# A shift by whole columns: read from DRAM at a computed place instead of multiplied by a matrix

## The chip, the cores and the metric

The kernel runs on one core of a Trainium2 chip. The metric is the device time of one execution in microseconds (us). The engines are called as in the profile: PE is TensorE, DVE is VectorE, ACT is ScalarE, POOL is GpSimd, SP is SyncE, whose queue issues almost all transfers (DMA) of this kernel. All arithmetic is in f32.

## The reference

Four layers follow each other on x with shape (32, 192, 56, 56). Each adds the result of a convolution-like block to x, and each block reads x through a group norm (32 groups of 6 channels, mean and variance over the 6 channels and all pixels of an image).

```python
x = x + _L0_conv_ref(_gn(x), ...)   # attention over 49 agents per image, 6 heads
x = x + _L1_conv_ref(_gn(x), ...)   # a scan over the 3136 pixels, forwards and backwards
x = x + _L2_conv_ref(_gn(x), L2_conv_offset)
x = x + _L3_conv_ref(_gn(x), ...)   # a 55x55 filter per channel, through a Fourier transform
```

Layer 2 is the one that the change is about. Its 48 positions own four channels each. A position has an offset in x and y; its whole part R shifts the image, with zeros where the source lies outside, and its fraction gives a 3x3 filter, a product of a column part and a row part, that is applied to the shifted image:

```python
R = jnp.round(offset); Ri = R.astype(jnp.int32)
y_src = jnp.arange(Hn)[None, :] - Ri[:, 1:2]
x_src = jnp.arange(Wn)[None, :] - Ri[:, 0:1]
out = where the source exists: inp[:, :, y_src, x_src], else 0
delta = offset - R
sq = (f[None, None, :] + delta[:, 0, None, None]) ** 2 + (f[None, :, None] + delta[:, 1, None, None]) ** 2
kern = jnp.exp(-sq / (2.0 * SIGMA ** 2)); kern = kern / kern.sum(axis=(1, 2), keepdims=True)
out_LO = depthwise convolution of out with kern, padding 1
```

The offsets are an input of the kernel, so the place is known only when it runs.

## The kernel before

The program has three long parts on the same core, one after the other. `attention` does layer 0 image by image, from about 300 to 5200 us of the span (before it, `make_filter` turns the filter of layer 3 into `spectra`). `scan_pairs` does layer 1 in pairs of images, up to about 8300 us, and writes its result to a tensor `x2` in DRAM, laid out by channel. `channel_blocks` does layers 2 and 3 channel by channel in the rest. It is called the channel stage here.

**Layout.** A channel of `x2` is a tile of 114 partitions: for each of two interleaved sets of images, 56 rows and one more row that holds the image's group mean (spread by the scan). Along the free axis lie 16 images of 56 columns each, 896 numbers. `rs2` holds the norm's factor for each channel and image.

**Shift (`shift`).** Two matrices, made on POOL once for each position (`matrices`, every fourth channel), carry shift, filter and zeros: one for rows (`diff_y`, then multiplied on PE by the fixed matrix `lags`, which subtracts the mean row, `L1550`, and copied by DVE, `L1552`), one for columns (`diff_x`). Each matrix takes three taps (`L1542`) and two additions (`L1546`, `L1547`) on POOL. A channel is then taken through PE twice, two interleaved images at a time: eight matmuls (`L1589`) give the rows shifted and the image turned, with columns on the partitions; DVE multiplies this by the norm's factor on its way out of PSUM (`L1596`); eight more (`L1607`) shift the columns and turn it back; DVE adds it to x (`L1615`) and sums x (`L1616`) for the next norm.

**Norm of layer 3 (`centre`).** DVE subtracts the mean into `padded` (`L1633`), ACT squares (`L1635`), DVE sums the squares (`L1636`); PE adds over the six channels of a group (`means`, `L1624`).

**Layer 3.** `analyse` takes `padded` to spectra (PE `L1757`, ACT copies `L1763`, PE `L1655`) and DVE multiplies with the filter's spectrum in six operations for each of three batches (`L1662` to `L1668`). `synthesise` goes back (PE `L1681` with ACT copies `L1688`, PE `L1698`), DVE multiplies by the norm's factor (`L1700`) and adds to x (`L1701`), and SP stores two halves of the channel (`L1704`).

**Order of the work.** The loop runs over 32 groups of six channels, with six steps each. In a step, one channel of the group before is analysed, the one before that is synthesised, and the present group has two shifts (steps 0 to 2) or two centrings (steps 3 to 5). The parts are generators and a written list says how they alternate:

```python
two = [shift(q, 2 * j + i) if j < 3 else centres(q, 2 * j - 6 + i) for i in range(2)]
for step in (taking, two[0], two[0], taking, ending, ending, two[0], taking, ...):
    next(step, None)
```

The framework may then reorder instructions on each engine within what the data and the buffers allow; every engine works through its own list in order. PSUM has eight banks here: four of the tag `ps`, shared by shift, `analyse` and `synthesise`, and two each for `re` and `im`. There are 15 buffers for x.

Of the kernel before, what the change touches and what calls it, by code (L numbers as in the profile page):

```python
# [67 lines left out]

def _resize_matrix():

    at = (np.arange(S) + 0.5) * POOL / S - 0.5
    w = np.maximum(0.0, 1.0 - np.abs(at[:, None] - np.arange(POOL)[None, :]))
    return w / w.sum(1, keepdims=True)
# [5 lines left out]
    (114, (114,)), (112, (112,)), (114, (2,)),  # L79
# [3 lines left out]
def _constants():  # L83
# [16 lines left out]
    for t in range(2):  # L100
# [17 lines left out]
        "chan_k": _filled([f[n] for n in "f1 f2 f3 f4 ones_rows lags diff_y diff_x at_rows".split()]),  # L118
# [3 lines left out]
def _spectral_constants():  # L122
# [21 lines left out]
    for s in range(2):  # L144
# [7 lines left out]
    col = np.arange(2 * S) % S  # L152
    together = np.arange(2 * S)[:, None] // S == np.arange(2 * S)[None, :] // S
    diff_x = np.where(together, col[None, :] - col[:, None], 1e6)
    at_rows = np.stack([np.concatenate([col, [0, 0]]), row], 1)
# [8 lines left out]
        "diff_x": diff_x,  # L164
        "at_rows": at_rows,
# [199 lines left out]
def attention(ctx: ExitStack, tc: tile.TileContext, a, ready, x1, st_a, st_c):  # L365
# [48 lines left out]
    for t in (*agents_b[0], *agents_b[1], v_a, v_c):  # L414
        nc.gpsimd.memset(t, 0.0)

# [342 lines left out]
    for b in range(NB):  # L759
# [28 lines left out]
        for t in range(1, NK + 2):  # L788
# [21 lines left out]
            if more and t == 4:  # L810
                o[0] = convolve(0)
                normed(nxt, rs, nb, 3)
        nc.sync.dma_start(out=st_a[:, b % 2, b // 2], in_=st[:, 0])
# [37 lines left out]
def scan_pairs(ctx: ExitStack, tc: tile.TileContext, a, k, x1, st_a, st_c, x2, rs2, count):  # L851
# [86 lines left out]
    kept_a, kept_c = small("kept_a", [128, 2, NB // 4, 2]), small("kept_c", [128, 2, NB // 4])  # L938
# [261 lines left out]
    def conclude(s):  # L1200
# [3 lines left out]
        nc.vector.tensor_copy(kept_a[:, p % 2, p // 2, :], rs[:, 0:2, 0])  # L1204
        nc.vector.tensor_copy(kept_c[:, p % 2, p // 2 : p // 2 + 1], rs[:, 2])
# [46 lines left out]
    for i, r in enumerate((slice(0, 64), slice(64, 128))):  # L1252
        nc.sync.dma_start(out=rs2[128:C, :, :, i], in_=kept_c[r])
# [17 lines left out]
def scan_guarded(ctx: ExitStack, tc: tile.TileContext, a, k, x1, x2, rs2):  # L1271
# [45 lines left out]
    kept = cp.tile([T, 2, 2, NB // 4, 2], F32, name="kept", tag="kept")  # L1317
# [47 lines left out]
    for b in range(NB):  # L1365
# [84 lines left out]
        g, i = b // 4, b // 2 % 2  # L1450
        nc.vector.tensor_copy(kept[:, :, i, g, b % 2], rs)
# [11 lines left out]
def channel_blocks(ctx: ExitStack, tc: tile.TileContext, a, k, x2, rs2, spectra, out):  # L1463
# [30 lines left out]
    f1, f2, f3, f4, ones, lags, diff_y, diff_x, at = pieces  # L1494
# [3 lines left out]
    for t in padded:  # L1498
        nc.gpsimd.memset(t[:, :, S:64], 0.0)

# [17 lines left out]
    ok = cp.tile([PR, NP, 2], F32, name="ok", tag="ok")  # L1518
    for d in range(2):
        nc.vector.tensor_scalar(ok[:, :, d], rnd[:, :, d], at[:, d : d + 1], None, ALU.add)  # L1520
    low = cp.tile([PR, NP, 2], F32, name="low", tag="low")
# [3 lines left out]
    nc.vector.tensor_tensor(gs, gs, _bc(ok.rearrange("p n d -> p (n d)"), [PR, NP * 2, 3]), ALU.mult)  # L1525
    where = cp.tile([PR, NP * 2, 3], F32, name="where", tag="where")
    for f in range(3):
        nc.vector.tensor_scalar(where[:, :, f], rnd.rearrange("p n d -> p (n d)"), float(1 - f), None, ALU.add)
# [3 lines left out]
    def matrices(n):  # L1532

        if n in made:
            return made[n]
        got = []
        for d, diff in ((1, diff_y), (0, diff_x)):
            r, m = diff.shape
            t = [wp.tile([r, m], F32, name=f"tap{d}{f}", tag=f"tap{d}{f}", bufs=1) for f in range(3)]
            for f in range(3):  # L1540
                i = 2 * n + d
                nc.gpsimd.tensor_scalar(  # L1542
                    t[f], diff, where[:r, i, f : f + 1], gs[:r, i, f : f + 1], ALU.is_equal, ALU.mult
                )
            mat = wp.tile([r, m], F32, name=f"mat{d}", tag=f"mat{d}", bufs=3)
            nc.gpsimd.tensor_tensor(t[0], t[0], t[1], ALU.add)  # L1546
            nc.gpsimd.tensor_tensor(mat, t[0], t[2], ALU.add)  # L1547
            if d == 1:
                ps = pp.tile([128, BANK], F32, name="ps", tag="ps", bufs=4)
                nc.tensor.matmul(ps[:PR, :PR], lags, mat, start=True, stop=True)  # L1550
                mat = wp.tile([r, m], F32, name="mat2", tag="mat2", bufs=3)
                nc.vector.tensor_copy(mat, ps[:PR, :PR])  # L1552
            got.append(mat)
        made.clear()
        made[n] = got
        return got
# [7 lines left out]
    def begin(n):  # L1564
        q = Group()
        q.n, q.x, q.padded = n, [], []
        q.scale = sp.tile([2 * S, GROUP, NG, 2], F32, name="scale", tag="scale")
        for i in range(2):
            nc.sync.dma_start(
                out=q.scale[S * i : S * (i + 1)], in_=rs2[n * GROUP : (n + 1) * GROUP, i].partition_broadcast(S)  # L1570
            )
# [4 lines left out]

    def shift(q, j):

        c = q.n * GROUP + j
        rows, cols = matrices(c // 4)  # L1580
        x = xp.tile([PR, NI, S], F32, name="x", tag="x")
        nc.sync.dma_start(out=x, in_=x2[c].rearrange("s h g w -> (s h) g w"))
        flat = x.rearrange("p g w -> p (g w)")
        turned = wp.tile([2 * S, NG, 2, S + 1], F32, name="turned", tag="turned")
        for g0 in range(0, NG, 4):
            n = min(4, NG - g0)
            ps = psum()
            for g in range(n):
                nc.tensor.matmul(  # L1589
                    ps[: 2 * S, g * PR : (g + 1) * PR],  # L1590
                    flat[:, (g0 + g) * 2 * S : (g0 + g + 1) * 2 * S],
                    rows,
                    start=True,
                    stop=True,
                )
            nc.vector.tensor_tensor(  # L1596
                turned[:, g0 : g0 + n].rearrange("p g s h -> p (g s) h"),
                ps[: 2 * S, : n * PR].rearrange("p (g h) -> p g h", h=S + 1),
                _bc(q.scale[:, j, g0 : g0 + n].rearrange("p g s -> p (g s)"), [2 * S, 2 * n, S + 1]),
                ALU.mult,  # L1600
            )
        yield
        for g0 in range(0, NG, 4):
            n = min(4, NG - g0)
            ps = psum()
            for g in range(n):
                nc.tensor.matmul(  # L1607
                    ps[:PR, g * 2 * S : (g + 1) * 2 * S],
                    turned[:, g0 + g].rearrange("p s h -> p (s h)"),
                    cols,  # L1610
                    start=True,
                    stop=True,
                )
            xc = flat[:, g0 * 2 * S : (g0 + n) * 2 * S]
            nc.vector.tensor_tensor(xc, xc, ps[:PR, : n * 2 * S], ALU.add)  # L1615
# [15 lines left out]
    def centre(q, j):  # L1631
        t = padded[(q.n * GROUP + j) % len(padded)]
        nc.vector.tensor_tensor(t[:, :, 0:S], q.x[j], _bc(q.mean, [PR, NI, S]), ALU.subtract)  # L1633
        sq = wp.tile([PR, NI, S], F32, name="sq", tag="sq")
# [73 lines left out]
    def centres(q, j):  # L1708
# [5 lines left out]
        yield  # L1714
# [3 lines left out]
    before, ending = None, iter(())  # L1718
    for n in range(C // GROUP + 1):
        q = begin(n) if n < C // GROUP else None  # L1720
        for j in range(GROUP):
# [4 lines left out]
            for step in (  # L1726
                taking, two[0], two[0], taking, ending, ending, two[0], taking, ending, ending, two[1], two[1], taking,
                ending, two[1], ending,
            ):
                next(step, None)  # L1730
            for rest in (*two, taking, ending):
# [37 lines left out]
def all_blocks(ctx: ExitStack, tc: tile.TileContext, a, k, out):  # L1769
# [7 lines left out]
    x1, x2 = scratch("x1", [NB, C, N]), scratch("x2", [C, 2, S + 1, NB // 2, S])  # L1777
# [118 lines left out]
```

## Time and profile before

| | us |
|---|---|
| median of 3 runs | 12296.9 |
| lowest and highest | 12290.89, 12297.15 |
| the profiled execution, its own time | 12294.66 |
| its span, from first to last instruction | 12292.8 |
| mean granted clock of TensorE | 0.966 |

| busy share of the span | PE | weight loads | DVE | ACT | POOL |
|---|---|---|---|---|---|
| whole program | 92% | 58% | 88% | 50% | 18% |

The 16 DMA engines moved 719.69 MB in 930055 packets, of which 770325 were under 512 bytes. The page gives each engine's busy time in 40 slices of the span (one slice is 307 us); the channel stage begins in slice 28. In it the granted clock is 1.00 (window 9000 to 11000 us). Lines such as `L1589` are lines of the kernel before. In groups of instructions the last columns are busy us, mean ns of one, idle time of the engine just before them and what ended it; in a timeline the first two columns are start and duration in us. An f32 matmul shows as two records.

### The profile page before, as it was taken

The numbers are of one execution on the slowest core, as the hardware profiler recorded it, in microseconds if no ns is written. First come the engines' busy times: TensorE is split into PE (matmuls) and PEld (weight loads), VectorE is DVE, ScalarE is ACT, GpSimd is POOL, SyncE is SP. The second block draws the span as 40 slices with busy tenths as digits, with TensorE's granted clock in tenths as the row PEclk, the third lists the DMA queues.
The fourth block names the chain that finished last, engine by engine and source line by source line (L and its number), as shares of the span: only waits on it lengthen the run. The fifth ranks groups of instructions, "written<-read, shape, count | busy, mean of one in ns | idle before, by whom it ended". The sixth has DMA issues, their size and how long they took to land. (4 is left out here: it accounts for less than half of the span.)

```text
span 12292.8 us, 164375 instructions
## 1 busy us (share of the span) xinstructions
PE 11329.2 (92%) x62734; PEld 7107.7 (58%) x62734; DVE 10836.4 (88%) x15489; ACT 6205.0 (50%) x11808; POOL 2250.7 (18%) x2228
## 2 busy tenths in 40 slices
PE   7999999999999999788888888888999999999999
PEld 3555555655555555333333333336777777777777
DVE  6888888888888887999999999997888888888888
ACT  3555555555555554566666666663333333333333
POOL 0000000000000000655555555551000000000000
PEclk9999999999999999999999999999999999999999
DMA  2111111111111111244344433442111111111111
GB/s 69 40 42 46 52 41 40 40 40 40 40 40 40 42 50 44 75 103 100 95 97 103 101 94 97 103 101 65 44 41 45 41 44 42 44 42 44 42 43 29
DMA packets 930055, 719.69 MB, mean 59 GB/s; under 512 B 770325, under 2 KB 807236, under 8 KB 920124
## 3 DMA queue, kind: packets, MB, share of 16 engines
q1 hardware_dynamic: 919020, 683.39, 21.7%
q10 hardware_dynamic: 10240, 25.70, 0.8%
q8 instruction: 500, 8.19, 0.3%
q14 instruction: 295, 2.42, 0.1%
HBM read 403.47 MB, written 240.65 MB: 52 GB/s over the span
## 5 line engine op out<-in xcount | busy, mean ns | idle before, releaser
L572 DVE SCALAR_TENSOR_TENSOR o<-v_a,att_w,o 128x896 f32<-128x896 f32 (+1 forms) x1024 | 1053.8, 1029 | 418.6 <-ACT v_a L546 291.5
L1763 ACT COPY y<-ps 64x252 f32<-64x252 f32 (+1 forms) x2376 | 808.2, 340 | 1135.0 <-PE ps L1757 1104.8
L1681 PE MATMUL ps<-fixed,real 84*84 84x112 f32 x6144 | 1090.9, 259 | 0.0
L1681 PE MATMUL ps<-fixed,imag 84*84 84x112 f32 x6144 | 1089.5, 259 | 0.0
L1688 ACT COPY z<-ps 84x448 f32<-84x448 f32 x768 | 405.6, 528 | 1218.5 <-PE ps L1681 1217.0
L1086 POOL MEMSET f<- 128x1 f32 x96 | 8.9, 99 | 4726.3 <-DMA st_c<-st 4721.3
L1681 PEld LDWEIGHTS ps<-fixed,real 84*84 84x84 f32 x6144 | 784.0, 153 | 134.2 <-issue 95.8
L1681 PEld LDWEIGHTS ps<-fixed,imag 84*84 84x84 f32 x6144 | 763.8, 153 | 0.0
L1079 ACT ACTIVATE q<-q 128x784 f32<-128x784 f32 x384 | 328.2, 855 | 802.5 <-DVE q L1074 633.1
L834 PE MATMUL ps<-sq,fixed 128*128 128x392 f32 x512 | 297.3, 743 | 428.6 <-ACT sq L1157 428.6
L572 DVE SCALAR_TENSOR_TENSOR o<-v_c,att_w,o 128x448 f32<-128x448 f32 (+1 forms) x1024 | 635.0, 620 | 5.1
L585 PE MATMUL ps<-xs_a,gk_a 128*98 128x448 f32 (+1 forms) x1536 | 637.1, 495 | 0.0
L589 ACT ACTIVATE pr<-ps,low 98x896 f32<-98x896 f32 (+1 forms) x384 | 352.3, 918 | 559.9 <-DVE low L587 559.9
L586 PE MATMUL ps<-xs_c,gk_c 125*98 125x448 f32 (+1 forms) x1536 | 631.6, 492 | 0.0
L1547 POOL TENSOR_TENSOR mat<-tap,tap 114x114 f32<-114x114 f32 x96 | 40.8, 425 | 3166.1 <-PE ps L1607 2313.2
L677 PE MATMUL ps<-gq_a,xs_a 128*112 128x294 f32 x1792 | 602.8, 417 | 19.2 <-DVE pq L682 19.2
L1698 PE MATMUL ps<-z,fixed 84*114 84x448 f32 x1536 | 608.8, 539 | 0.0
L834 PE MATMUL ps<-x,weights 128*128 128x392 f32 x1536 | 577.4, 519 | 27.5 <-DVE bv L1108 14.2
L678 PE MATMUL ps<-gq_c,xs_c 125*112 125x294 f32 x1792 | 594.5, 412 | 0.0
L1655 PE MATMUL re<-y,fixed 128*84 128x420 f32 (+1 forms) x1152 | 532.3, 543 | 8.7 <-ACT y L1763 7.6
L1655 PE MATMUL im<-y,fixed 128*84 128x420 f32 (+1 forms) x1152 | 526.9, 538 | 0.0
L690 ACT ACTIVATE pq<-pq 112x1176 f32<-112x1176 f32 x224 | 265.3, 1184 | 498.9 <-DVE pq L682 376.0
(367 smaller groups left out, 29245.2 us busy)
## 6 DMA issues: line engine op xcount, KB each, us to landing
x<-x SPq DMA_DIRECT2D x576, 392.0 KB
x<-x SPq DMA_DIRECT2D x512, 196.0 KB
x<-x SPq DMA_DIRECT2D x192, 399.0 KB
out_x<-x SPq DMA_DIRECT2D x384, 196.0 KB
x<-in_x SPq DMA_DIRECT2D x32, 1568.0 KB
x<-x SPq DMA_DIRECT2D x32, 1568.0 KB
x<-in_x SPq DMA_DIRECT2D x64, 392.0 KB
rd<-rd ACTq DMA_DIRECT2D x128, 196.0 KB
```

The source lines that it names most:

```text
L572: nc.vector.scalar_tensor_tensor(dst, tap(i), dww[:, t, i : i + 1], dst, ALU.mult, ALU.add)
L585: mm(ps[P2, h, :n], g[:, cols], xs_a[j][:, px], start=True, stop=False)
L586: mm(ps[P2, h, :n], gk_c[0:KC, 2 * j + h, cols], xs_c[j][0:KC, px], start=False, stop=True)
L589: nc.scalar.activation(pr[:, :, :n], ps[P2, :, :n], AF.Exp, bias=low[:, j, p : p + 1], accum_out=sums[:, j, p : p + 1])
L677: mm(ps[:SUB, i, :HA], xs_a[j][:, px], g, start=True, stop=False)
L678: mm(ps[:SUB, i, :HA], xs_c[j][0:KC, px], gq_c[0:KC, 2 * j + (q + i) // ns], start=False, stop=True)
L834: mm(out, aa, srcs[t][h], start=True, stop=False)
L1655: nc.tensor.matmul(ps[:, : n * 84], f2[:, i, :], y[:, i0 : i0 + n].rearrange("p g s u -> p (g s u)"), start=True, stop=True)
L1681: nc.tensor.matmul(ps[:84, i * 2 * S : (i + 1) * 2 * S], part[:, i0 + i].rearrange("p s u -> p (s u)"), f3[:, m, :], start=(m == 0), stop= ...
L1688: nc.scalar.copy(z[:, i0 : i0 + n].rearrange("p g m w -> p (g m w)"), ps[:84, : n * 2 * S])
L1698: nc.tensor.matmul(got, f4[:, m, :], z[:, i0 : i0 + n, m, :], start=(m == 0), stop=(m == 1))
L1763: nc.scalar.copy(y[64 * m : 64 * m + 64, 2 * g0 + i : 2 * (g0 + n) : 2], got[64 * i : 64 * i + 64, :, :, m, :])
```

## The change

The columns are no longer shifted by a matrix. `x2` is now one flat tensor in DRAM in which each row of 56 numbers is followed by 56 zeros (`PITCH`), with 64 zeros ahead and behind (`LEAD`). A whole channel read from a start moved by R columns is then the channel shifted by R columns, with zeros coming in. The zeros (`gaps`) are written by 192 DMAs in `attention`, six behind each image's code.

For each channel a new function `prepare` runs four channels ahead: SP loads the start from SBUF into a register once for each position, a DMA reads the channel from the computed place into one of three buffers `shifted`; POOL multiplies it by the norm's factor (`scale`, now laid out by images on the free axis); ACT multiplies it by the three column taps, each with its own scale (`y`, then twice `more`, from a shared set of three buffers `spare`, which the squares of `centre` use too); POOL adds the three into `smooth`. In `shift`, PE applies the row matrix with two matmuls of 448 columns, and DVE adds the result to x. x itself is loaded too, as before, but from the layout with gaps. The row matrix (`matrix`) is made as before, the column matrix falls away, and with it the multiplication on DVE (`L1596`). The list of steps loses one turn for each shift. `kept_a`, `kept_c`, `kept` and `rs2` follow the new order of images.

```diff
+PITCH = 2 * S
+LEAD = 64
...
+    for at in (0, x2.shape[0] - LEAD):
+        nc.sync.dma_start(out=x2[at : at + LEAD].unsqueeze(0), in_=zeros[0:1])
...
+        for c in range(C * b // NB, C * (b + 1) // NB):
+            nc.sync.dma_start(
+                out=gaps[c].rearrange("s h g w -> (s h) g w"),
+                in_=zeros[:, 0:S].unsqueeze(1).to_broadcast([2 * (S + 1), NB // 2, S]),
+            )
...
+    shifted = [cp.tile([PR, NI, S + 2], F32, name=f"shifted{i}", tag=f"shifted{i}") for i in range(3)]
+    for t in shifted:
+        nc.gpsimd.memset(t, 0.0)
...
+    begins = cp.tile([1, NP], I32, name="begins", tag="begins")
+    nc.vector.tensor_scalar(begins, rnd[0:1, :, 0], -1.0, float(LEAD), ALU.mult, ALU.add)
...
+    def prepare(c):
...
+        n, j = divmod(c, GROUP)
+        if j == 0:
+            scales[n] = sp.tile([PR, GROUP, NI], F32, name="scale", tag="scale", bufs=3)
...
+        i = c // 4
+        if c % 4 == 0:
+            begin_at[i] = nc.values_load(
+                begins[0:1, i : i + 1], engines=(mybir.EngineType.SP,), min_val=LEAD - S, max_val=LEAD + S
+            )
+        t = shifted[c % len(shifted)]
+        there = flat_x2[bass.ds(begin_at[i] + c * SPAN, SPAN)].rearrange("(p g w) -> p g w", p=PR, w=PITCH)
+        nc.sync.dma_start(out=t[:, :, 1 : S + 1], in_=there[:, :, 0:S])
+        nc.gpsimd.tensor_tensor(t, t, _bc(scales[n][:, j], [PR, NI, S + 2]), ALU.mult)
+        y = wp.tile([PR, NI, S], F32, name="smooth", tag="smooth", bufs=5)
+        taps = [gs[:, 2 * i, f : f + 1] for f in range(3)]
+        nc.scalar.activation(y, t[:, :, 0:S], AF.Copy, scale=taps[0])
+        for f in (1, 2):
+            more = wp.tile([PR, NI, S], F32, name="more", tag="spare", bufs=3)
+            nc.scalar.activation(more, t[:, :, f : f + S], AF.Copy, scale=taps[f])
+            nc.gpsimd.tensor_tensor(y, y, more, ALU.add)
+        smooth[c] = y
+
     def shift(q, j):
...
-        for g0 in range(0, NG, 4):
...
-                nc.tensor.matmul(
-                    ps[: 2 * S, g * PR : (g + 1) * PR],
-                    flat[:, (g0 + g) * 2 * S : (g0 + g + 1) * 2 * S],
-                    rows,
...
-            nc.vector.tensor_tensor(
-                turned[:, g0 : g0 + n].rearrange("p g s h -> p (g s) h"),
...
-                nc.tensor.matmul(
-                    ps[:PR, g * 2 * S : (g + 1) * 2 * S],
-                    turned[:, g0 + g].rearrange("p s h -> p (s h)"),
-                    cols,
...
+        for g0 in range(0, NI, 8):
+            n = min(8, NI - g0)
+            px = slice(g0 * S, (g0 + n) * S)
             ps = psum()
+            nc.tensor.matmul(ps[:PR, : n * S], rows, y[:, px], start=True, stop=True)
+            nc.vector.tensor_tensor(flat[:, px], flat[:, px], ps[:PR, : n * S], ALU.add)
         nc.vector.tensor_reduce(q.sums[:, 0, j, :], x, AX.X, ALU.add)
...
+    for c in range(4):
+        prepare(c)
...
+            prepare(n * GROUP + j + 4)
...
+    n = C * 2 * (S + 1) * (NB // 2) * PITCH
+    x1, flat = scratch("x1", [NB, C, N]), scratch("x2", [n + 2 * LEAD])
+    wide = flat[LEAD : LEAD + n].rearrange("(c s h g w) -> c s h g w", c=C, s=2, h=S + 1, w=PITCH)
+    x2, gaps = wide[..., 0:S], wide[..., S:PITCH]
```

## The prediction

> **What bounds the kernel now.** I read the 40 slices of the page first: PE reads 9 over the last third, which is the channel stage. Then the busy times of an undisturbed stretch of that stage, the groups in the same stretch by shape, and PE's timeline.
>
> ```profile
> PE   7999999999999999788888888888999999999999
> DVE  6888888888888887999999999997888888888888
> POOL 0000000000000000655555555551000000000000
> ```
>
> The next line holds a window, its length, then the busy us of PE, weight loads, DVE, ACT and POOL, the granted clock, the DMA share and GB/s.
>
> ```profile
> 9000.00:11000.00 2000.00, 1975.96 (x13516) 1525.41 (x13515) 1737.21 (x2917) 714.49 (x1718) 164.00 (x245) 1.00 0.17 43
> ```
>
> One reduction `L1616` belongs to one channel and it counts 99, so a channel takes 2000/99 = 20.2 us: PE works 99% of it, DVE 17.55 us, ACT 7.2, POOL 1.7. PE sets the pace. The starts of `L1757` in PE's timeline, one per step of the loop, stand 23.2, 23.2, 23.2, 17.6, 16.4 and 17.7 us apart: three steps with two shifts each, three with two centrings each, 121.3 us for a group of six channels, 32 groups.
>
> ```profile
> 10012.46 1.74 PE L1589 MATMUL ps<-mat,x 114*112 114x114 f32 x16
> 10014.22 1.02 PE L1607 MATMUL ps<-mat,turned 112*114 112x112 f32 x8
> 10015.08 1.01 PE L1655 MATMUL re<-y,fixed 128*84 128x504 f32 x2
> 10015.93 0.96 PE L1607 MATMUL ps<-mat,turned 112*114 112x112 f32 x8
> 10016.73 1.01 PE L1655 MATMUL im<-y,fixed 128*84 128x504 f32 x2
> 10017.58 3.17 PE L1698 MATMUL ps<-z,fixed 84*114 84x448 f32 x8
> 10020.58 2.44 PE L1757 MATMUL ps<-fixed,padded 114*128 114x168 f32 x16
> ```
>
> From start to start: `L1589` holds PE 1.76 us, `L1607` 0.86 + 0.80 = 1.66 us. Eight records with 448 columns (`L1698`) hold it 3.00 us, so 0.375 each; an f32 matmul is two records.
>
> **PE's part of the change.** Per channel 16 small matmuls (3.42 us) go and two with 448 columns come (4 x 0.375 = 1.50 us): 1.92 us less, 3.84 in a step with two shifts. The lags matmul stays. PE's floor for a group is 3 x (23.2 - 3.84) + 51.7 = 109.8 us against 121.3; if all of it arrived, 32 x 11.5 = 368 us.
>
> **DVE, ACT, POOL, DMA.** These rows are the groups of the same 2000 us by shape (last numbers: busy us, mean ns).
>
> ```profile
> L1596 DVE TENSOR_TENSOR turned<-ps,scale 112x456 f32<-112x456 f32 x198 | 124.2, 630 | 107.8 <-PE ps L1589 107.8
> L1701 DVE TENSOR_TENSOR x<-x,o 114x448 f32<-114x448 f32 x198 | 123.6, 624 | 1.9
> L1664 DVE TENSOR_TENSOR real<-a,a 84x420 f32<-84x420 f32 x199 | 117.7, 591 | 0.0
> L1633 DVE TENSOR_TENSOR padded<-x,mean 114x896 f32<-114x896 f32 x99 | 106.9, 1080 | 0.6
> L1635 ACT ACTIVATE sq<-padded 114x896 f32<-114x896 f32 x99 | 94.1, 951 | 37.3 <-DVE padded L1633 35.7
> L1542 POOL TENSOR_SCALAR tap<-fixed,where,gs 112x112 f32<-112x112 f32 x72 | 65.3, 912 | 5.0
> L1546 POOL TENSOR_TENSOR tap<-tap,tap 114x114 f32<-114x114 f32 x25 | 10.7, 428 | 0.0
> ```
>
> DVE loses `L1596`: 124.2/99 = 1.25 us per channel, leaving 16.3, or 97.8 per group: about 16.4 us in a step with shifts, 16.2 in one with centrings (two shifts keep 4.6 us in `L1615` and `L1616`, two centrings 4.3 in `L1633` and `L1636`). ACT gains three passes over 114x896 at 0.95 (`L1635`), 2.9 us: 10.1 of 18 us, room enough in sum. POOL loses the three taps and two adds of the column matrix every fourth channel, and gains per channel one multiplication over 928 and two additions over 896 elements. The trace has no such long POOL operation. A one-element copy of the scan takes 0.18 us where nothing stands beside it, the addition over 114 takes 0.428; that makes 2.2 ns an element, so 2.13 us for 896 and 2.2 for 928. Bounds: 0.83 us from the memset `L302` (952 ns for 1024, no reads) and 3.4 us with 428 ns in full proportion. I take 2.13, since it separates the fixed part. POOL then works 6.5 us plus 0.8 for the row matrix, 7.3 of some 18 per channel: no bound as a sum.
>
> Each channel gets a second load of x2, now in runs of 224 bytes like the output stores. DMA is busy 17% in this stage; with the x load in runs of 224 bytes too, a channel then has three transfers of the stores' kind instead of one, and the stores are now some 10 of the 17%: about 35%, hidden. In the order of SP they stand behind output stores that wait for `L1701`'s addition; they run at least two steps ahead of their use. The 192 zero fills of the attention stage (399 KB each) run while DMA is at 16%, but some 36 to 42 of them stand in one row on SP ahead of `gk_c`, needed once per image (146 us): I price that, with the longer first chain load, POOL, ACT, POOL, PE, at 25 us; 0 and 60 are the ends.
>
> **The shared wait.** What decides is where POOL and DVE touch. The scan shows it: line, count, then ns least/median/most.
>
> ```profile
> L1073 POOL COPY b<-p x157: 185/1662/2577, 5599.5 to 8298.0; 128x1 f32<-128x1 f32 x157
> L1664 DVE TENSOR_TENSOR real<-a,a x298: 579/582/702, 9001.9 to 10999.4; 84x420 f32<-84x420 f32 x99, 84x504 f32<-84x504 f32 x50
> ```
>
> One element is copied in 0.185 us or, typically, in 1.66, ending as a DVE operation with two inputs in SBUF ends. The other way round, `L1664` (two SBUF inputs) rises from 0.582 to 0.70 only when it begins 0.2 us after a tap of POOL. [...]
>
> In numbers of this trace: DVE has nine operations with two SBUF inputs per channel (`L1664` and `L1668` three each, `L1701` two, `L1633`), 597/99 = 6.0 us, so between two of them lie (16.3 - 6.0)/9 = 1.14 us of other work. If a POOL operation of 2.13 us holds off the next one to its end, as DVE's hold off the copies, that one loses 2.13 - 1.14 = 1.0 us. Ends: 0.12 (`L1664`) and 2.13 (all of it). I take 1.0, because the 0.12 was lost beside an operation over 112 elements, not 896.
>
> Where they fall matters. In the order of the changed kernel POOL's 18 long operations of a group are not spread: ten fall into the first step with shifts, two into the other two, six into the steps with centrings. DVE in the first step: 16.4 + 10 = 26.4 us, above PE's 19.4. ACT agrees: five passes named `more` stand ahead of that step's twelve copies of `y`, held by their three buffers until POOL's additions free them (the fifth may write only after two additions, 5.2 us), and a later one stands ahead of a copy of `z`; walking that chain with 2.3 us per POOL operation gives a first step of some 24 us, so the two explanations overlap and I count the larger. The next two steps: PE's 19.4 each. Centring steps: 16.2 + 2 = 18.2 against PE's 17.2. Sum 26.4 + 38.8 + 54.6 = 119.8. Two engines so close lose to each other: the stage loses 0.24 us per channel now with PE well ahead, I add 0.3, 1.8 per group. 121.6 against 121.3: 32 x 0.3 = 10 us more, and 25 from above. The profiled execution took 12294.66 us (span 12292.8), 2.2 under the median of 12296.9. Forecast 12294.7 + 35 = 12330 us. With 0.7 to 1.3 us per operation (first step not under 24.2) its own range is 12200 to 12480.
>
> **Rivals.** *PE stays the bound* (faster). POOL delays DVE by 0.12 us as at `L1664`, and the ACT chain costs the first step 3.6 us: 23 + 38.8 + 51.7 = 113.5, minus 7.8 x 32 = 250, plus 25: about 12070; all of PE's saving gives 11950. For it: the only row in which DVE waits for POOL is small, and DVE has 2 us to spare per channel. Against it: the copies. It decides once the delay is below 0.5 us per operation (DVE then 21.4 us in the first step, 17.2 in the centring ones).
>
> [...] POOL's next operation is issued before the waiting DVE operation gets its turn, as `L1073` shows copies of 2577 ns that wait out more than one DVE operation. At 1.6 us per operation: 32.4 + 38.8 + 58.2 + 1.8 = 131.2, plus 317 + 25: 12640; at 2.13, 12890. It decides from 1.3 us on.
>
> *The shifted copy comes late*: SP's in-order queue puts its load behind a store, and PE waits for it. One lost step per group would be 18 x 32 = 580 us; the two steps of lead speak against it.
>
> **Chances.** Forecast 0.45, PE bound 0.27, POOL again 0.25, late copy 0.03. The measurement tells about 0.2% (25 us) from no change. Faster: 0.27 and 0.10 of the forecast's low part, 0.37; same 0.08; slower 0.55. Range 12000 to 12680: about 0.07 of the PE case lies below, 0.12 of the slow ones above.
>
> **What would show it.** Right: `L1664`, `L1668` and the addition into x with means well above 0.59 and 0.62; a POOL addition near 2.1 us; first step of a group near 26 us, centring steps near 18; PE under 95% busy. PE at 98% with steps of 19.4 and 17 would refute the shared wait; DVE's means doubled would make the second rival. Wrong altogether: waits of the `smooth` matmul for DMA, or an attention stage longer by over 60 us.

## The result, and the profile after

The changed kernel takes 12731.8 us (median, 12730.91 to 12735.85) against 12296.72 us beside it: a ratio of 1.0356, interval 1.0338 to 1.0374. That is 435 us slower. The forecast was 12330 us, with a range of 12000 to 12680. Each kernel's runs lie within 7 us of each other.

The 40 slices of the page after, to be held against those of before: PE reads 5, 4, 4 in the second to fourth slice, where it read 9. That is the attention stage, which the change touches only with the zero fills. In the last third PE reads 8 and 9, DVE has risen to 9, and POOL reads mostly 3 and 4, where it read 0.

```profile
PE   7544999999999999978888888887899999999999
DVE  6444888888888888799999999997899999999998
POOL 0000000000000000055555555554533433433330
```

The profiled execution (span 12729.3 us, before 12292.8) splits by the starts of four instructions: the first scan operation (`L1072` before, `L1080` after), the first matmul with the row matrix and `lags` (`L1550`, `L1556`), and the first and the last of the 192 steps. A step begins with the forward DFT's matmul (`L1757`, `L1767`).

| stretch | before, us | after, us | difference |
|---|---|---|---|
| start to the first scan operation (attention) | 4919.3 | 5429.4 | +510 |
| from there to the first matmul with `lags` | 3466.7 | 3460.2 | -7 |
| from there to the first step | 35.0 | 70.8 | +36 |
| first step to last step | 3839.7 | 3736.5 | -103 |
| rest | 32.1 | 32.4 | 0 |

**The attention stage.** The first line below is a group of the page: its last part is PE's idle time in front of `L589`, 451 us (0.0 in front of the same matmul before), and what ended it. The second view is the DMA queue of SP: start, us, instruction, how many. The third is the same queue before.

```profile
L589 PE MATMUL ps<-xs_c,gk_c 125*98 125x448 f32 (+1 forms) x1536 | 637.9, 496 | 451.0 <-DMA gk_c<-once 451.0
```

```profile
515.42 0.94 SPq L522 DMA_DIRECT2D gq_c<-once  x1
516.42 217.83 SPq L817 DMA_DIRECT2D x<-zeros  x37
734.35 5.79 SPq L522 DMA_DIRECT2D gk_c<-once  x1
```

```profile
647.38 0.92 SPq L519 DMA_DIRECT2D gq_c<-once  x1
766.54 0.89 SPq L519 DMA_DIRECT2D gk_c<-once  x1
```

37 zero fills stand between the load of `gq_c` and that of `gk_c`, and SP is 218 us in getting rid of them, 5.8 us each. In the queue of before 119 us lie between these two loads, so there was cover for some 119 us. PE waits for `gk_c` in four of the first images, for 128, 108, 105 and 105 us, 446 in all: the loads of `gk_c` stand 280, 268, 268, 263 and 154 us apart, then mostly 146.7 us as before. What the other 64 of the 510 us are is not split further; the granted clock from 480 to 760 us is 0.77, where it was 0.97.

**The channel stage.** An undisturbed stretch, with the columns of the line that the prediction shows: PE has fallen from 1976 to 1889 us, DVE has risen from 1737 to 1868, POOL from 164 to 749, the DMA share from 0.17 to 0.31. PE sets the pace no longer.

```profile
9000.00:11000.00 2000.00, 1889.25 (x11001) 1315.35 (x11000) 1868.34 (x2786) 1028.85 (x2070) 749.29 (x436) 0.98 0.31 66
```

One group, step by step, in the same columns:

```profile
10147.70:10171.70 24.00, 21.40 (x110) 13.65 (x110) 23.86 (x29) 13.42 (x25) 21.32 (x11) 0.93 0.48 103
10171.70:10193.10 21.40, 19.65 (x111) 13.25 (x110) 19.25 (x31) 8.26 (x18) 6.57 (x7) 1.00 0.23 50
10193.10:10212.50 19.40, 19.15 (x109) 13.09 (x108) 16.60 (x29) 7.23 (x17) 0.00 (x0) 1.00 0.21 43
10246.40:10264.90 18.50, 17.43 (x114) 12.89 (x112) 18.46 (x28) 10.93 (x22) 7.55 (x4) 1.00 0.32 65
```

These are the three steps with shifts and the last one with centrings. In the first POOL works 21.3 us and DVE is full (23.86 of 24.00). In the third POOL does nothing, and PE's matmuls take nearly the whole step: 19.4 us, the floor of the prediction. The groups by shape of another 2000 us show who pays; the last two lines are the 84x504 forms before:

```profile
L1608 POOL TENSOR_TENSOR smooth<-smooth,more 114x896 f32<-114x896 f32 x204 | 461.0, 2263 | 948.7 <-ACT more L1607 933.8 <-ACT smooth L1604 6.5
L1709 DVE TENSOR_TENSOR x<-x,o 114x448 f32<-114x448 f32 x204 | 190.2, 932 | 2.3
L1672 DVE TENSOR_TENSOR real<-a,a 84x504 f32<-84x504 f32 x102 | 126.4, 1239 | 0.0
L1676 DVE TENSOR_TENSOR imag<-a,a 84x504 f32<-84x504 f32 x102 | 118.9, 1165 | 0.0
L1670 DVE TENSOR_TENSOR a<-re,g 84x504 f32<-84x504 f32 x102 | 68.4, 670 | 0.0
```

```profile
L1668 DVE TENSOR_TENSOR imag<-a,a 84x504 f32<-84x504 f32 x99 | 66.3, 670 | 0.0
L1664 DVE TENSOR_TENSOR real<-a,a 84x504 f32<-84x504 f32 x99 | 66.3, 669 | 0.0
```

`L1672`, `L1676` and `L1709` read both inputs from SBUF and rise (`L1709` from 624 to 932 ns, the 84x504 forms from 670 ns to about 1.2 us). `L1670`, of the same size but with one input in PSUM, stays at 670.

### The profile page after: what moved, and what is told of

It reads as the page before. It is cut to its first block, busy times and chain, and to the rows that moved or that the text cites. A ratio compares the mean times of both kernels' runs of the same rounds, so it can differ in the third digit from the quotient of the medians.

```text
span 12729.3 us, 155334 instructions
## 1 busy us (share of the span) xinstructions
PE 11101.3 (87%) x57358; PEld 6648.0 (52%) x57358; DVE 10982.8 (86%) x15105; ACT 6753.3 (53%) x12384; POOL 3332.2 (26%) x2568
## 5 line engine op out<-in xcount | busy, mean ns | idle before, releaser
L1608 POOL TENSOR_TENSOR smooth<-smooth,more 114x896 f32<-114x896 f32 x384 | 865.4, 2257 | 1675.1 <-ACT more L1607 1644.3
L589 PE MATMUL ps<-xs_c,gk_c 125*98 125x448 f32 (+1 forms) x1536 | 637.9, 496 | 451.0 <-DMA gk_c<-once 451.0
L590 DVE TENSOR_REDUCE low<-ps 98x1 f32<-98x896 f32 (+1 forms) x384 | 365.3, 965 | 466.5 <-PE ps L589 464.9
L589 PEld LDWEIGHTS ps<-xs_c,gk_c 125*98 125x98 f32 x1536 | 254.0, 166 | 709.7 <-DMA gk_c<-once 454.7
L1767 PE MATMUL ps<-fixed,padded 114*128 114x168 f32 x3072 | 503.0, 312 | 73.2 <-DVE o L1708 58.1
```

The costliest lines, as they stand in the source:

```text
L589: mm(ps[P2, h, :n], gk_c[0:KC, 2 * j + h, cols], xs_c[j][0:KC, px], start=False, stop=True)
L1608: nc.gpsimd.tensor_tensor(y, y, more, ALU.add)
L1767: nc.tensor.matmul(ps[:, g * 168 : (g + 1) * 168], flat[:, (g0 + g) * 128 : (g0 + g + 1) * 128], f1, start=True, stop=True)
```

## Experiments

**Theories.** A: the 510 us of the attention stage are the zero fills, and their length comes from their shape (114 partitions): the queue spreads such a transfer over few DMA engines (an estimate, 7.5 engines' work, from 1824 packets of 24 ns in 5.8 us). Its rival: fills cost by their bytes or their number. B: in the channel stage each long POOL operation that reads SBUF holds up DVE's operations with two SBUF inputs, by some 0.8 us. Its rivals: any POOL work does so; or what costs is ScalarE's line behind POOL.

### The fills alone

The kernel before, with the 192 fills into a tensor that nothing reads:

```
...
+        for c in range(C * b // NB, C * (b + 1) // NB):
+            nc.sync.dma_start(
+                out=gaps[c].rearrange("s h g w -> (s h) g w"),
+                in_=zeros[:, 0:S].unsqueeze(1).to_broadcast([2 * (S + 1), NB // 2, S]),
+            )
...
```

> The kernel before, with the 192 zero fills of the change added to attention (same shape, same place in the code) into a tensor of its own that nobody reads. Theory: the whole loss of the attention stage, 510 us between the starts of the scan, comes from the fills, which stand in SP's queue ahead of gk_c and take 5.8 us each; then about 12297 + 500 = 12800 us, with four images of some 265 us instead of 147. Rival: part of the loss comes from the new layout or from the other new work; then the fills alone cost clearly less than 450 us.

Measured: 12789.4 us, ratio 1.0405 (1.0384 to 1.0426). PE's idle time before the same matmul is the changed kernel's to within a microsecond, and so are the distances of the `gk_c` loads (280, 259, 268, 259, 154 us); the channel stage is that of before (121.2 us a group). From the start to the first scan operation it takes 5416.7 us, 497 more than before: 497 of the 510 us are the fills'. What the other 13 are is not shown.

```profile
L587 PE MATMUL ps<-xs_c,gk_c 125*98 125x448 f32 (+1 forms) x1536 | 638.6, 496 | 450.7 <-DMA gk_c<-once 450.7
```

### The same zeros from 128 partitions

The changed kernel, with the same rows of 224 bytes dealt out as 171 fills over 128 partitions instead of 192 over 114:

```
...
+        rows = gaps.rearrange("c s h g w -> (c s h g) w")
+        for i in range(171 * b // NB, 171 * (b + 1) // NB):
             nc.sync.dma_start(
...
+                out=rows[2048 * i : 2048 * (i + 1)].rearrange("(p g) w -> p g w", g=16),
+                in_=zeros[:, 0:S].unsqueeze(1).to_broadcast([128, 16, S]),
             )
```

> The changed kernel with the same zeros written by 171 fills over 128 partitions (2048 runs of 224 bytes each) in place of 192 over 114 partitions (1824 runs). Theory A: a fill takes 5.8 us because its runs are not spread over all 16 DMA engines (1824 packets at the measured 24 ns are 43.8 us of engine time, so 5.8 us keep only 7.5 engines busy); spread over 16, a fill takes 2048 x 24 / 16 = 3.1 us, the longest row of 41 takes 126 us, and attention's loss falls from 510 to under 40 us: about 12240 us. Theory B: SP or the queue needs 3.2 ns per run whatever the shape; then 6.5 us per fill and nothing gained, 12730 us or a little more. [...]

Measured: 12219.1 us, ratio 0.9941 (0.9924 to 0.9957), 0.6% faster than before. The first scan operation starts at 4923.9 us, 5 later than before. A fill takes 2.43 us at the median. The queue of SP has 37 fills in a row again, ahead of the same load, but they are gone in 99 us and nobody waits:

```profile
502.26 0.93 SPq L522 DMA_DIRECT2D gq_c<-once  x1
503.24 99.38 SPq L818 DMA_DIRECT2D x<-zeros  x37
621.72 0.93 SPq L522 DMA_DIRECT2D gk_c<-once  x1
```

```profile
L589 PE MATMUL ps<-xs_c,gk_c 125*98 125x448 f32 (+1 forms) x1536 | 631.6, 492 | 0.0
```

The bytes in all, the length of a run and the place in the queue are the same, and 37 fills stand in the row both times, so the length comes from the shape, as A has it, and the price by bytes or number falls (5.8 us for 399 KB, 2.43 for 448). How many packets are under way at once can be read from the windows of the two rows, narrow fills first, wide ones below (the last but one number is the DMA share; at 1.05 packets overlap):

```profile
517.00:734.00 217.00, 106.17 (x593) 66.38 (x591) 104.06 (x166) 58.91 (x103) 0.00 (x0) 0.75 0.49 77
503.00:602.00 99.00, 94.00 (x600) 62.70 (x600) 94.00 (x146) 47.88 (x82) 0.00 (x0) 0.95 1.05 187
```

In numbers: a narrow fill has 1824 packets of 24 ns, and 43.8 us of packets in 5.8 us is 7.5 of them under way at once. The DMA shares above give 0.49 x 16 = 8 in the narrow row and 1.05 x 16 = 17 in the wide one. Half as many at once is shown. The packets of the trace do not name their engine, so that the narrow fill used fewer engines is the author's estimate from these shares; how many it used is not shown.

### The narrow fills, each image's own behind that image

The changed kernel, with the zeros of an image written by POOL from that image's statistics, so that its six fills can't run ahead:

```
...
+        still = small("still", [2 * (S + 1), S])
+        nc.gpsimd.tensor_scalar(still, st[0 : 2 * (S + 1), 0, 0:1].to_broadcast([2 * (S + 1), S]), 0.0, None, ALU.mult)
...
-                in_=zeros[:, 0:S].unsqueeze(1).to_broadcast([2 * (S + 1), NB // 2, S]),
+                in_=still.unsqueeze(1).to_broadcast([2 * (S + 1), NB // 2, S]),
...
```

> The changed kernel with each image's six fills tied to that image: their zeros are made from the image's own statistics (times 0), so that they can't be issued before. Theory: only their bunching ahead of gk_c costs; six fills of 5.8 us are 35 us in an image of 147 us, hidden; attention's loss falls from 510 to under 30 us, about 12240 us. Rival: the fills' traffic slows attention's own transfers wherever it runs; then the same total comes back, spread over 32 images, 12600 us or more.

Measured: 12429.5 us, ratio 1.0113 (1.0096 to 1.013), between the two expectations. The clump is gone, but six fills still stand right ahead of `gk_c` in each image:

```profile
1526.64 28.95 SPq L819 DMA_DIRECT2D x<-still  x6
1555.71 5.60 SPq L522 DMA_DIRECT2D gk_c<-once  x1
```

Most images take some 153.5 us instead of 146.8, and 32 x 6.7 = 214 us is about the distance from the wide fills (210 us). Here, spreading the fills in time was worth less than dealing them out over 128 partitions.

### One addition less

The changed kernel (narrow fills), with the second POOL addition left out; the third tap is then missing from the output.

```
-            nc.gpsimd.tensor_tensor(y, y, more, ALU.add)
+            if f == 1:
+                nc.gpsimd.tensor_tensor(y, y, more, ALU.add)
```

> The changed kernel without POOL's second addition per channel (the third column tap is still computed by ACT, but left out of the sum). Theory of the shared wait: DVE's two-input operations wait out POOL's; POOL's long operations per channel fall from three to two, so the first two steps of a group (23.9 and 22.0 us) lose about a third of their excess over PE's 19.4 or more, the last step goes from 18.4 towards 17.7, the group from 117.8 to some 114, the program by 100 to 130 us. Rival: the chain of ACT's three buffers sets the first step; an addition less frees a buffer at once, so the first step falls to about 20 while the means of the DVE operations (1239, 1165 and 932 ns) stay.

Measured: 12546.4 us in one run. The group falls from 117.8 to 112.0 us (20.07, 20.11, 19.50, 17.58, 16.32, 18.41). The first step now has five long POOL operations instead of ten. In one group, DVE's eight two-input operations of that step sum to 9.19 us, against 13.19 with ten and 4.92 with none: 0.85 and 0.83 us for each. Over the 27 middle groups, each operation counted against its time alone (582, 670, 618 and 1077 ns by shape), the price in the first step is 0.74 with five and 0.79 with ten. Over all steps it is 0.54 and 0.70 us for each long POOL operation. The longest wait that any of these operations shows is 1.94 us, less than one addition of POOL (2.26). The same operations, fewer neighbours (84x504 `imag` was 1165, `real` 1239, x plus o 932):

```profile
L1710 DVE TENSOR_TENSOR x<-x,o 114x448 f32<-114x448 f32 x214 | 135.5, 633 | 2.5
L1673 DVE TENSOR_TENSOR real<-a,a 84x504 f32<-84x504 f32 x107 | 132.3, 1237 | 0.0
L1677 DVE TENSOR_TENSOR imag<-a,a 84x504 f32<-84x504 f32 x107 | 87.1, 814 | 0.0
```

The gain, 185 us, is larger than the 100 to 130 of the theory, and the first step fell to about 20 us, as the rival had it. Two of the three means fell, against the rival. DVE was full in the first step with ten operations (23.3 of 23.9 us on the mean), so its waits suffice for the length of that step; that the line of ScalarE behind POOL would not have given the same length is not shown.

### POOL busy without reading

The changed kernel (narrow fills), with both additions left out and nine small fills in place of each:

```
-            nc.gpsimd.tensor_tensor(y, y, more, ALU.add)
+            for _ in range(9):
+                blank = wp.tile([PR, 3, S], F32, name="blank", tag="blank", bufs=1)
+                nc.gpsimd.memset(blank, 0.0)
```

> The changed kernel with its narrow zero fills, with both GpSimd additions of a channel left out and nine small fills of zeros each put in their place, which write about as many elements but read none; the columns are then weighted with one tap only. GpSimd keeps as many instructions or more in the same places. If what costs VectorE is any work of GpSimd, its two-input operations keep means of about 1.2 us in the first step (84x504) and the step stays at 23 to 24 us. If it is only GpSimd operations that read two inputs, the 84x504 means fall to about 0.7 us, the first step to 19.4 to 20.1 us (TensorE's), the last step to about 16.4 us, and the group to about 110 us, with a time near 12731 - 32 x 7.8 = 12480 us.

Measured: 12746.7 us in one run, not 12480. The small fills depend on nothing, so they did not stay in their places: all 3456 ran before 10058 us, in the first nine of the 32 groups, which took 137 to 146 us each from the second on. That makes two clean stretches. With POOL full of fills (663.66 of 800 us busy, 577.5 of them with fills), DVE's two-input operations keep the durations that they had before (669 and 624 ns for the two below):

```profile
9200.00:10000.00 800.00, 651.15 (x3614) 450.57 (x3615) 551.19 (x917) 340.03 (x690) 663.66 (x2501) 0.88 0.26 54
```

```profile
L1674 DVE TENSOR_TENSOR real<-a,a 84x504 f32<-84x504 f32 x34 | 22.8, 670 | 0.0
L1711 DVE TENSOR_TENSOR x<-x,o 114x448 f32<-114x448 f32 x68 | 42.1, 619 | 0.8
```

And after them, with POOL's multiplication by the factor as the only long operation left, a group takes 110.6 us (20.1, 19.5, 19.5, 17.6, 16.3, 17.6): PE's floor, put at 109.8 in the prediction. Among the fills one form grew, `real` at 84x420, from 591 to 646 ns; POOL's multiplications, which read, were still running there. So the fills, which only write, cost DVE nothing here, and the additions, which read, do (0.70 us each in the changed kernel): of these two it is the one that reads that costs. A fill is short (238 ns); a long operation that only writes was not tried. The expected means and group came, the expected time did not.

### Places of their own

`more` and `sq` share three places, taken in program order; so the `more` passes stand behind the squares of the centring steps, and POOL's additions pile up in the next group's first step. On top of the wide fills:

```
...
-            more = wp.tile([PR, NI, S], F32, name="more", tag="spare", bufs=3)
+            more = wp.tile([PR, NI, S], F32, name="more", tag="more", bufs=2)
...
-        sq = wp.tile([PR, NI, S], F32, name="sq", tag="spare", bufs=3)
+        sq = wp.tile([PR, NI, S], F32, name="sq", tag="sq", bufs=1)
```

> The kernel with the wide zero fills, and one thing more: the tap products (more) and the squares (sq) no longer take turns in three shared places, but have two places and one place of their own. In the order on ScalarE the two tap products of a channel then follow its first one, in the three shift steps, where they now come bunched behind the squares of the centring steps; GpSimd's eighteen long operations of a group should so lie six to each shift step instead of ten in one. Theory (each long GpSimd operation costs VectorE's two-input operations 0.83 us, wherever it lies, and shift steps have slack up to TensorE's 19.4 us): shift steps of about 16.4 + 6 x 0.83 = 21.4 us, centring steps of 16.3 us, 113 us a group instead of 117.8, and 12219 - 32 x 4.8 = 12065 us (12000 to 12130). Rival (the bunch is not what costs, the group's length comes from the order of the steps on VectorE): 117.8 us a group stays and the time is 12200 to 12240 us.

Measured: 12152.4 us, ratio 0.9886 (0.987 to 0.9903); the group takes 115.0 us: 19.56, 20.86, 20.85, 19.75, 16.33, 17.66. Of the eighteen long operations 4.6, 6.0, 5.9 and 1.5 now fall in the first four steps, and the sum of the three shift steps is 61.3 us instead of the 64 expected: the price there is 0.6 us for each operation (over the 27 middle groups), not 0.83. The expectation's centring steps were wrong: 16.3 is the shortest of three, which before sum to 51.6, and 61.3 + 51.6 = 112.9. The remaining 2.1 us are in the first centring step (17.6 before). Spreading the operations helps, by less than the forecast, and the version beats both kernels. PE is now busy 111.1 of the 115.0 us.

Four variants looked for those 2 us. Two places for the squares:

> As the kernel with places of their own for the tap products and the squares, but the squares have two places instead of one, and x has fourteen instead of fifteen. It tells whether the single place of the squares holds ScalarE back in the centring steps. If it does, the centring steps are shorter than in that kernel, by up to 1 us each, and the time is up to 100 us less; if VectorE bounds these steps, as it does now (16.2 us busy of 16.3), the times agree within 20 us.

Measured: 12162.9 us, 10 us from the version before, within the 20; the squares hold nothing back. Three, then four places for `more` (`bufs=3` and 14 places for x, `bufs=4` and 13):

> The kernel with places of their own, with three places for the tap products instead of two (x has fourteen). There ScalarE stood before each tap product for 1.6 us on average until GpSimd's addition had freed a place, and its copies z and y, for which TensorE and VectorE wait, stood in line behind. Theory (the rest of the distance from 115.0 us a group to the forecast 113 is this hand-over): the wait falls below 0.5 us for each, the group to about 113 us and the time to 12152 - 32 x 2 = 12090 us (12050 to 12130). Rival (what is left is VectorE's price for each long GpSimd operation, which the places do not change): 115 us a group and 12150 us within 20.

> The same with four places for the tap products, so that two channels' worth fit, and thirteen for x. If the hand-over between ScalarE and GpSimd still costs with three places, this takes the rest away: the time is at or under that with three. If VectorE's price for each long operation is what is left, it is within 20 us of it. If thirteen places for x are too few, a step waits for the store of a channel and the time is above it by more than 30 us.

Measured: 12165.5 and 12159.5 us, the groups 115.4 us. The times are the rival's. ScalarE's wait for POOL's additions is as long as ever: in the same 2000 us 341.8 us (210 times) with two places, 336.0 (204) with three, 340.6 (208) with four. It is a wait for a place all the same: of 384 tap products 376 begin when they take the second and last place, 365 the third of three, 356 the fourth of four. With more places ScalarE runs further ahead and then waits at the pace at which POOL frees them. So the places do not set the time; that VectorE's price does, as the rival says, is not shown by this.

Four places for the shifted copy (`for i in range(4)`, 14 for x, 2 for `more`):

> The kernel with two places of their own for the tap products, with four places for the shifted copy of a channel instead of three (x has fourteen). More places for the tap products changed nothing; in the chain of work that ended last of that kernel the shifted load has 7.3 %, about 8 us of a group of 115 us, against 3.3 % in the changed kernel. Theory (a place of the shifted copy comes free late, the load starts late and its landing is on the path): the load leaves the chain, the shift steps lose 0.5 to 1 us each, the group comes to about 113 us and the time to 12152 - 32 x 2 = 12090 us (12040 to 12130). Rival (the chain only passes through the load because GpSimd's next operation is in step with it; VectorE's price remains): 115 us a group and 12150 us within 20.

Measured: 12146.8 us, ratio 0.9882 (0.9865 to 0.9898), 114.6 us a group. The time is the rival's again: the load's share of the chain rose from 7.3 to 9.8% instead of leaving it. In the chain of that version PE's lines have the largest shares (`L1690` alone 21.1%).

What makes the first centring step some 2 us longer than before stays open. In the version with places of its own PE works 18.8 us in it (17.4 before) and DVE 18.4 (16.1 before): work of the shift steps runs over into it.

### A third addition

The version with places of its own, with one more POOL addition per channel, first with two places for `more`, then with three. The first writes its result to a tile of its own, the second over `more`:

```
+            if f == 1:
+                blank = wp.tile([PR, NI, S], F32, name="blank", tag="blank", bufs=1)
+                nc.gpsimd.tensor_tensor(blank, y, more, ALU.add)
```

```
+            if f == 1:
+                nc.gpsimd.tensor_tensor(more, y, more, ALU.add)
```

> The kernel with places of their own, with a third long GpSimd addition for each channel, whose result nothing reads: 24 long operations in a group instead of 18, eight in a shift step. Theory (a price of 0.83 us for VectorE for each, where VectorE sets the pace): 16.4 + 8 x 0.83 = 23.0 us for a shift step, 5 us more for a group than with 18, and some 160 us more in all. Rival (GpSimd's work is hidden once it is spread evenly, since it is then 17 us busy in a step of 21): the group and the time stay within 1 us and 30 us.

> The kernel with three places for the tap products, and a third long GpSimd addition for each channel, whose result nothing reads (it is written over the tap product). With two places the third addition cost 13.3 us a group instead of the forecast 5, and ScalarE's waits for GpSimd grew to 3.9 us a channel at the added operation. Theory (a price of 0.83 us on VectorE for each, the rest was ScalarE's line behind the waits): with three places the third addition costs 5 to 8 us a group over the kernel without it. Rival (GpSimd's own chain of five long operations for a channel sets the pace of the shift steps, 20 us busy of 25): 11 us or more as before.

Measured: 12567.8 us and 128.3 us a group, 12613.8 us and 129.4, one run each: 13.3 and 14.0 us more for six operations. Both expectations for the first missed; for the second the rival holds. With the third addition the price in the long shift steps is 0.83 and 0.86 us for each operation. In the two long shift steps of one group of the second version (24.86 and 24.50 us) DVE works 23.9 and 23.1 us, PE 21.1 and 21.4, POOL 17.8 and 20.0. In the centring step behind them, 24.3 us long, neither is full: DVE works 20.8 and PE 20.7. The chain of the second, by line, names POOL first, which the chain without the third addition does not have among its leading lines:

```profile
by line: POOL smooth L1609 16.3%; PE ps L1692 15.6%; POOL more L1611 8.1%; PE re L1666 7.3%; ACT y L1776 7.2%; PE im L1666 6.7%; PE ps L1625 5.8%; PE ps L1709 4.8%; ACT smooth L1605 3.9%; ACT more L1608 3.1%; PE ps L1635 2.4%; PE ps L1770 2
```

So the price is not one number: the versions have 0.54 to 0.86 us on the mean. In the shift steps DVE's part came out as the theory has it (16.4 + 8 x 0.86 = 23.3 us, 23.4 busy). But the centring step behind them, which neither DVE nor PE fills, grew from some 20 us to 24 and 25, and the chain runs through POOL first. That POOL's own chain sets the pace at 24 operations fits this, but no run shows it alone.

## Why the prediction was wrong, by its own steps

**The zero fills: the step that failed.** The prediction put the fills, together with the longer first chain, at 25 us, 0 and 60 being the ends. It saw "some 36 to 42 of them stand in one row on SP ahead of `gk_c`", and took the rest from the DMA share of 16%. It never multiplied that row by the duration of a fill, nor set it against the time between the two loads. 37 fills of 5.8 us, 218 us with what lies between them, against 119 us of cover is 100 us for each of four images; PE waited 446 us there, and the stage lost 510, 497 of them with the fills alone. The row was right, the duration of a fill was the missing term, and the trace of before has none. The nearest transfers there, the two stores of a channel with 1792 runs of 224 bytes (from 9517 us on), move in 2.7 us, and 37 x 2.7 = 100 us would have fitted under the cover, as the wide fills do (37 in 99 us). So the size hung on how much of a fill is under way at once (8 packets narrow, 17 wide, by the DMA shares), which the prediction did not ask for. Its own sign of being "Wrong altogether", an attention stage longer by over 60 us, is what came.

**The first chain** was in the same 25 us, and cost 36 by itself. PE waits 20.3 us for the first `smooth`. For about half of that POOL makes row matrices for later channels (`L1549` to `L1554`, 8894.6 to 8904.6 us), which stand ahead of the first additions in its list, while both tap products are there from 8897.6 us on. Then PE waits for POOL, which needs 5.9 us a channel while nothing else is there to do:

```profile
8904.63 1.74 POOL L1601 TENSOR_TENSOR shifted<-shifted,scale 114x928 f32<-114x928 f32 x1
8906.33 4.24 POOL L1608 TENSOR_TENSOR smooth<-smooth,more 114x896 f32<-114x896 f32 x2
```

**PE's part** was right: 19.4 us is the step in which POOL is silent, and 110.6 us the group without the additions, against the forecast floor of 109.8.

**The shared wait** was the right mechanism, with its price put too high: 1.0 us forecast for each long operation, 0.79 measured in the first step (0.83 in the group shown) and 0.70 over all steps, the low end of the stated 0.7 to 1.3. POOL's addition takes 2.26 us (2.13 forecast), the multiplication 1.94 (2.2). The runs show both sides: an addition into x that takes 0.62 us alone took 2.50 us beside POOL's additions (10150.92 us), and beside POOL's fills, which read nothing, it stayed at 0.62.

**The sum of the group** came out 121.6 against 117.8 measured. First step: 26.4 forecast, 23.9 measured, for 7.5 us of delay instead of 10 (16.4 + 7.5 = 23.9). Second step: 19.4 and 22.0; DVE works 19.6 us in it, against 16.7 in the third, so work of the first step runs on. That the three shift steps come to 65.2 us forecast and 65.4 measured is luck: two misses cancel. Centring steps: 18.2 each forecast, 17.6, 16.3 and 18.4 measured. Seven long operations fall there, but most of their delay is taken up where PE had the longer part, and only the last step grew (17.7 before). The 1.8 us for two engines so close can't be told apart in this. The change is worth 103 us in its own stage, less 36 at its start. With the wide fills little more is lost, and the 12219 us lie at the low end of the forecast's own range.

**The rivals.** The second rival, a POOL operation issued before the waiting DVE one gets its turn, gave 12640 us, the nearest number, and for the wrong reason: the channel stage got shorter, not longer, and its 1.6 us for each operation stands against 0.79 in the first step. (By its own terms its second figure, at 2.13 us, is 12908 and not 12890.) "PE stays the bound" gave 113.5 us a group, and its 0.12 us for each operation is refuted by 0.70. The late shifted copy did not come: POOL waited 136.4 us in 2000 for these loads, at most 3.2 at once.

## What to carry to other kernels

Transfers that were "hidden" by bandwidth still occupied the queue that issues them here (218 us for 37 fills, at a DMA share of 0.49): count those ahead of the next load that matters, multiply by the measured duration of one such transfer, and set it against the gap between the loads around it. Look at the partition count of a bulk DMA before thinking of its place: here 128 instead of 114 brought a fill from 5.8 to 2.43 us. When work moves to GpSimd, count its SBUF-reading operations against VectorE's two-input ones in each step (0.54 to 0.86 us for each long one here), and look at which step the buffers' rotation puts them into.

## What the hardware showed that was not expected

A row of waiting transfers showed on one that has nothing to do with them: the load of `gk_c` right behind the 37 narrow fills holds SP for 5.79 us, one that comes 19 us after the last of the 37 wide ones 0.93. And POOL's fills, which only write, left VectorE's 84x504 operations at 670 ns and its addition into x at 619 with POOL 83% busy, while POOL operations that read, at 2.26 us each, raised VectorE's two-input ones from 0.62 and 0.67 us to between 0.93 and 1.24 on the mean.
